# A conditioned block on one core: the first pair of batches in another order, weight sums stored in front of the last rows and x, and the last inner sum split over VectorE's queue

## The chip, the cores and the metric

The kernel runs on one core of a Trainium2 chip. The metric is the device time of one execution in microseconds; before the change the median of three runs is 465.22 us (464.73 to 466.36). The profile is of a further execution of its own, which took 467.79 us.

The engines are named as in the profile: PE is TensorE (matmuls; PEld its weight loads), DVE is VectorE, ACT is ScalarE, POOL is GpSimd, and SP is SyncE, which here only issues DMAs. A small q behind an engine (SPq, ACTq) marks its sequencer.

## What is computed

x has 32 batches of 128 tokens with 512 features, in float32. Each batch has a condition vector, from which two small products give a shift, a scale and a gate for each of two halves. The first half acts on masked tokens only; the second half acts on all tokens.

```python
m = mask[:, :, None]
emb = silu(t) @ ada_w + ada_b
shift, scale, gate_msa = split(emb, 3, axis=1)
norm = layernorm(x) * (1.0 + scale[:, None]) + shift[:, None]
norm = where(m, norm, 0.0)
fwd = gelu(norm @ ssm_w1 + ssm_b1) @ ssm_w2 + ssm_b2
bwd = flip(the same with bwd_w1 .. bwd_b2 on flip(norm, axis=1), axis=1)
x = x + gate_msa[:, None] * where(m, fwd + bwd, 0.0)
ff_ada = silu(t) @ ffada_w + ffada_b
shift_mlp, scale_mlp, gate_mlp = split(ff_ada, 3, axis=1)
ff_norm = layernorm(x) * (1.0 + scale_mlp[:, None]) + shift_mlp[:, None]
h = gelu_tanh(ff_norm @ ff_w1 + ff_b1)        # 512 -> 1024
out = x + gate_mlp[:, None] * (h @ ff_w2 + ff_b2)   # 1024 -> 512
```

The products act on each token alone, so the two flips cancel, and forward and backward become one product with the two weights side by side.

## The kernel before

**First half, on slots.** The masked tokens are counted and given numbers, the slots. Rows of x are gathered into 512 slots (four tiles of 128, `xc`), in two halves of 256. For each half, `hidden` (L182) computes eight tiles of gelu outputs, `project` (L196) multiplies them into one accumulator of 128 slots (eight matmuls, L202), and `keep_slots` (L299) does the rest: VectorE adds the bias (L208), multiplies by the gate (L210), adds `xc` (L301), and SP stores the rows in `x1_rows` in DRAM (L302). Slots 0 and 1 are done early. Slots 2 and 3 are computed while the second half of the kernel begins.

**Second half, in four pairs.** A pair is two sides of four batches (1024 tokens). x is loaded by SP into tiles of two batches (`load_side`, L325; the DMA is L331), and `take_first_half` (L671) then overwrites masked tokens by indirect gathers from `x1_rows` on GpSimd (L675), one for each batch; other tokens are out of bounds and stay. VectorE takes statistics (L707, L708), GpSimd the root (L713), VectorE normalises (L719) and transposes blocks of 32 by 32 in place. `turned` (L739) then brings features onto partitions with 16 DMAs of 64 KB in pieces of 128 bytes (L746), and `scaled` (L748) applies scale and shift by batch on ScalarE (L729, 16 instructions a side). In pair 0, side 1 is turned by TensorE (L735) and scaled by VectorE (L727) instead, between the matmuls of `project` for slot 3.

**Seven products instead of eight, twice.** Both products of a pair are done by Strassen's method in Winograd's form. In the first one it is used on two levels. The outer level has streams 1 to 7 (`STREAMS` gives the order 1, 2, 5, 6, 3, 7, 4). Within each, the products P1 to P7 are matmuls with 128 rows of contraction (L907), with sums taken in PSUM and by VectorE, GpSimd and ScalarE on the way. The outer sums of weights for streams 5, 6, 7 and 4 are made once by `weight_sums` (numbered 1, 2, 3 and 4), stored in DRAM (`t_rows`) by `store_weight_sums` (L586, DMAs L588 and L589, 512 and 384 KB), and loaded again for each pair by `load_weights` (L848, DMA L853). The inner sums of x are `TokenBlocks` (L757): `one(1)` to `one(4)` (L776), each one VectorE instruction of 128x1024. The outer sums of x are `token_sums` (L826: L836, L840, L843, L846).

`FirstProduct.phase` (L898) issues the matmuls of one product and what follows from it. What matters here:

- `seed` (L947) prepares the accumulator e from a: a ScalarE copy (L953) for stream 1, a VectorE sum (L951) for stream 2. P2 waits for it.
- After P6, VectorE puts a + P5 into e (L932). P7 and P3 follow.
- After P7 and P4, VectorE makes L937 and L942; after P2 and P3, ScalarE copies (L965) or applies gelu (L869).
- GpSimd makes the sums that cross streams: `with_p5` (L958) and `after` (L987), and `late_sum` (L991).

`SecondProduct` (L1015) does the second product on one level with the steps of `ORDER` (P1U, P5U, P1V, P5V, P2U, ...), 16 matmuls each (L1087). P5 needs block sums of gelu outputs: `first_block` (L1038, L1041), then for P6 the second block, which subtracts `ha` (L1106).

**What sets the order.** Each engine runs its instructions in the order in which the program lists them (the scheduler is set to manual at L364), and an instruction waits on semaphores for what it reads and for buffers to come free. DMAs of SP, ScalarE and GpSimd are issued from the engine's own queue, so a DMA that waits holds up everything behind it there. In steady state the order comes from `window` (L996), which runs the seven products of a new stream mixed with the last of the old, and from `fills`, a table of (window, place) with the functions to be called there. In pair 0 it is written out by hand (L1132 to L1211). Buffers come from pools: the pools `hp` and `gp` of the second half are opened only at L1185, in the space of the pool `ssm` of the first half, so their first writers (the weights' DMA L853 and the first writers of the gelu tiles) wait until the last reader of the tiles there is done.

The order around the change, by hand: five gathers of pair 0, statistics, three more gathers, the DMA of gate rows, the stores of weight sums 4 on GpSimd (L1132 to L1141); the transposes and DMAs of xT on SP and ScalarE, the table load, the 16 scalings; slot 2; slot 3 with the transposes of side 1 between its matmuls (L1173); the stores of weight sums 1 and 2 on SP and two x tiles of pair 1 (L1174, L1175); `one(1)`; slot 3's sum with `one(2)` and `one(3)` between L208 and L210; then the products.

Of the kernel before, what the change touches and what calls it, by code (L numbers as in the profile page):

```python
# [22 lines left out]
def kernel(  # L23
# [158 lines left out]
    def hidden(xT, n, w, bcol, func, name, pool, parts=range(HC)):  # L182

        h = []
        for f in parts:
            ph = ps_h.tile([P, 512], F32, tag="h", name=f"ph_{name}_{f}")
            for k in range(KC):
                nc.tensor.matmul(  # L188
                    ph[:, :n], w[:, k, ts(f, P)], xT[:, k, :], start=(k == 0), stop=(k == KC - 1)
                )  # L190
            t = pool.tile([P, n], F32, tag="h", name=f"h_{name}_{f}", bufs=HC + 2)
            nc.scalar.activation(t, ph[:, :n], func, bias=biasT[:, bcol + f : bcol + f + 1])  # L192
            h.append(t)
        return h
# [10 lines left out]
    def gated(po, bias, gate, name, between=lambda: None):  # L205

        t = tp.tile([P, D], F32, tag="t", name=f"t_{name}")
        nc.vector.tensor_tensor(t, po, bias, ALU.add)  # L208
        between()
        nc.vector.tensor_tensor(t, t, gate, ALU.mult)  # L210
        return t
# [84 lines left out]
    def finish_slots(at, h1, gate, between=None):  # L296
        keep_slots(at, project(at % (NC // 2), h1, w2, f"s{at}", between), gate)

    def keep_slots(at, po, gate, between=lambda: None):  # L299
        t = gated(po, b2, gate, f"s_{at}", between)  # L300
# [100 lines left out]
    slot_row = ssm.tile([P, NS], F32, name="slot_row")  # L401
# [184 lines left out]
    def store_weight_sums(*which, queue=nc.sync):  # L586
        for j in which:
            queue.dma_start(t_rows[j - 1, :, :4], t_sum[j][0])  # L588
            queue.dma_start(t_rows[j - 1, :, 4:], t_sum[j][1][:, :3])  # L589
# [76 lines left out]
    t = in_blocks(sp.tile([P, G, D], F32, tag="s12", name="tw_4"))  # L666
    t_sum[4] = [t[:, :4], t[:, 4:]]
# [347 lines left out]
    class SecondProduct:  # L1015
# [31 lines left out]

        def third_block(self, c):
# [20 lines left out]
        def step(self, step):  # L1069
# [33 lines left out]
            if product == "P5":  # L1103
                self.p5[c] = keep_and_seed((e, a), f"o{p}_{c}")

                nc.vector.tensor_tensor(s1[c], s1[c], ha[:, :hh, tok], ALU.subtract)  # L1106
# [25 lines left out]
    take_first_half(0, x_of[0], range(G + 1))  # L1132
    stats = [Statistics(x_of[0][side], f"0_{side}") for side in range(2)]
# [7 lines left out]
    store_weight_sums(4, queue=nc.gpsimd)  # L1141
# [24 lines left out]

    po_s2 = project(0, h1, w2, "s2")

    def keep_and_turn():
        keep_slots(2, po_s2, gs[0])  # L1170
        turn(2)()

    po = project(1, h1, w2, "s3", {0: turn(0), 1: turn(1), 2: keep_and_turn, 4: turn(3)})  # L1173
    store_weight_sums(1, 2)  # L1174
    x_of[1] = [load_side(1, 0, spare)]  # L1175
    of_x[0] = TokenBlocks(0, xT)
    of_x[0].one(1)

    def outer_sums():
        of_x[0].one(2)  # L1180
        of_x[0].one(3)

    keep_slots(3, po, gs[1], outer_sums)
# [6 lines left out]
    now.apart(1)  # L1190
    now.do(1, "P1")
# [3 lines left out]
    of_x[0].one(4)  # L1195
# [16 lines left out]
    for p in range(NP):  # L1212
# [25 lines left out]
        if more_pairs:  # L1238
            if p == 0:
                x_of[1].append(load_side(1, 1))  # L1240
# [19 lines left out]
            if p == 0:  # L1260
                put(2, 6, take_first_half, 1, x_next, range(2 * G))
            else:
                put(1, 6, take_first_half, p + 1, x_next, range(G))
                put(2, 6, take_first_half, p + 1, x_next, range(G, G + 2))
                put(3, 4, take_first_half, p + 1, x_next, range(G + 2, G + 3))
                put(5, 4, take_first_half, p + 1, x_next, range(G + 3, 2 * G))
# [16 lines left out]
        now.do(4, "P7")  # L1283
        if more_pairs:
            for i in range(2, G):
                blocks(0, i)
            to_feature_rows(0, nc.sync)
        second.step(1)
        now.do(4, "P4")
        second.load_gate(1)  # L1290
        for lo in (0, 2):
            second.first_block(1, lo, lo + 2)
# [169 lines left out]
```

## Time and profile before

| | us |
|---|---|
| Median of three runs (range) | 465.22 (464.73 to 466.36) |
| The profiled execution | 467.79 |
| Its span, first to last instruction | 466.0 |
| Busy in the span: PE / DVE / ACT / POOL | 451.4 / 330.8 / 175.4 / 160.0 |
| First matmul of the first half's last hidden stage | 59.08 |
| First matmul of pair 0's products | 88.42 |
| First matmul of pair 0's second product | 135.61 |
| First matmul of pair 1's products | 180.22 |

A line of a timeline gives start, length (of the whole run of like instructions), engine, line, operation, out<-in with the program's names, shape and count; in brackets the idle time of the engine before it, and what ended it. Matmuls are pipelined, so the start of a group says more than its end. A matmul of float32 shows as two records for each pair of operands, four in a group of two matmuls. In the windows view each row is a stretch of time, with the busy time and the number of instructions of PE, PEld, DVE, ACT and POOL, then the granted clock of TensorE, the mean busy share of the 16 DMA engines and GB/s.

### The profile page before, as it was taken

The page shows a single profiled execution, that of the slowest core. Times are in us where ns is not written, and L with a number is a line of the kernel's source. Part 1 is how long each engine was busy: PE and PEld are TensorE (multiplying, and loading weights), DVE is VectorE, ACT ScalarE, POOL GpSimd, SP SyncE. Part 2 cuts the span into 40 slices and gives each one's busy share as a digit, 9 for nine tenths or more (in the row PEclk, how much of TensorE's full clock was granted, in tenths as well). Part 3 has the DMA queues.
Part 4 walks back from the last instruction along what each step waited for, and adds up shares of the span by engine and source line. Part 5 has one row for each costly group of instructions (what it writes and reads, how often), then busy time and mean ns, then how long its engine had stood idle before and what let it go on. Part 6 is the DMA issues. An engine that isn't in the chain of part 4 may idle for free.

```text
span 466.0 us, 5828 instructions
## 1 busy us (share of the span) xinstructions
PE 451.4 (97%) x2000; PEld 365.3 (78%) x2000; DVE 330.8 (71%) x538; ACT 175.4 (38%) x380; POOL 160.0 (34%) x153
## 2 busy tenths in 40 slices
PE   6899999899999999999999999999999999999995
PEld 2385385477788888888888888888888888888884
DVE  4649768969668759996787399867864995434645
ACT  3121021734364371354553713444546144562000
POOL 6210074038973000389710004897000025660000
PEclk9999999989999999999999999999999999999999
DMA  8999716880406752834086438330973342212022
GB/s 277 386 407 355 302 50 140 265 316 22 165 0 198 102 108 86 291 118 162 1 209 101 98 107 313 98 136 3 235 100 73 127 168 79 80 68 114 0 79 105
DMA packets 82418, 70.41 MB, mean 151 GB/s; under 512 B 63168, under 2 KB 63696, under 8 KB 81362
## 3 DMA queue, kind: packets, MB, share of 16 engines
q1 hardware_dynamic: 67298, 57.03, 40.0%
q0 software_dynamic: 4480, 11.66, 7.4%
q10 hardware_dynamic: 10608, 1.32, 2.0%
q8 instruction: 17, 0.28, 0.3%
q14 instruction: 15, 0.12, 0.1%
HBM read 56.83 MB, written 13.17 MB: 150 GB/s over the span
## 4 chain that ended last, share of the span: by engine, by line
PE 74%; POOL 8%; ACT 5%; issue 5%; DVE 4%; DMA 3%; SPq 0%; POOLq 0%; DVEq 0%
PE a_o L1087 19%; PE e_o L1087 16%; PE a_m L907 14%; PE e_m L907 11%; PE ph_s L188 6%; PE po_s L202 4%; POOL hb L991 2%; ACT hb L869 2%; POOL x L675 2%; DMA x<-in_x_dram 2%; DMA tw<-t_rows 1%; POOL ha L958 1%; DVE xT L727 1%; ACT ha L869 1%; PE part_s L283 1%
## 5 line engine op out<-in xcount | busy, mean ns | idle before, releaser
L958 POOL TENSOR_TENSOR ha<-p_m,ha 128x512 f32<-128x512 f32 x20 | 27.4, 1369 | 152.5 <-ACT ha L965 143.3
L1087 PE MATMUL e_o<-fw,ha 128*128 128x256 f32 x256 | 57.9, 379 | 0.0
L729 ACT ACTIVATE xT<-xT,modT 128x128 f32<-128x128 f32 x112 | 44.2, 480 | 29.4 <-DMA xT<-xn 29.4
L1087 PE MATMUL a_o<-t,hb 128*128 128x256 f32 x240 | 54.1, 379 | 0.0
L1087 PEld LDWEIGHTS e_o<-fw,ha 128*128 128x128 f32 x256 | 48.6, 190 | 6.6
L1087 PEld LDWEIGHTS a_o<-t,hb 128*128 128x128 f32 x240 | 45.6, 190 | 6.2
L675 POOL DMA_INDIRECT x<-x_rows,slot_i x32 | 37.5, 1173 | 26.9 <-DMA x_rows<-t_s 18.6
L869 ACT ACTIVATE hb<-hb,biasT 128x256 f32<-128x256 f32 x64 | 29.0, 501 | 28.1 <-POOL hb L991 19.4
L958 POOL TENSOR_TENSOR hb<-p_m,hb 128x512 f32<-128x512 f32 x20 | 28.3, 1415 | 23.0 <-DVE e_m L951 22.7
L921 ACT COPY p_m<-e_m 128x512 f32<-128x512 f32 x27 | 15.8, 586 | 50.1 <-PE e_m L907 50.1
L1087 PE MATMUL e_o<-fw,s 128*128 128x256 f32 x128 | 29.2, 381 | 0.5 <-DVE s L1041 0.3
L965 ACT COPY ha<-e_m 128x512 f32<-128x512 f32 x32 | 18.5, 579 | 28.5 <-PE e_m L907 26.9
L1087 PE MATMUL a_o<-fw,ha 128*128 128x256 f32 x128 | 28.9, 379 | 0.0
L1087 PE MATMUL a_o<-t,s 128*128 128x256 f32 x128 | 28.9, 379 | 0.0
L202 PE MATMUL po_s<-w,h_s 128*128 128x512 f32 x64 | 28.6, 592 | 0.0
L188 PE MATMUL ph_s<-xT_s,w 128*128 128x256 f32 x128 | 28.6, 382 | 0.0
L1087 PEld LDWEIGHTS e_o<-fw,s 128*128 128x128 f32 x128 | 24.1, 190 | 4.8 <-DVE s L1041 1.7
L188 PEld LDWEIGHTS ph_s<-xT_s,w 128*128 128x128 f32 x128 | 24.0, 190 | 4.7 <-ACT h_s L192 1.5
L1087 PEld LDWEIGHTS a_o<-t,s 128*128 128x128 f32 x128 | 24.3, 190 | 3.3
L1087 PEld LDWEIGHTS a_o<-fw,ha 128*128 128x128 f32 x128 | 24.3, 190 | 3.3
L932 DVE TENSOR_TENSOR e_m<-a_m,ha 128x512 f32<-128x512 f32 x20 | 13.9, 696 | 17.6 <-POOL ha L958 7.4
L869 ACT ACTIVATE ha<-e_m,biasT 128x256 f32<-128x256 f32 x48 | 20.1, 469 | 15.8 <-PE e_m L907 8.9
(207 smaller groups left out, 872.3 us busy)
## 6 DMA issues: line engine op xcount, KB each, us to landing
tw<-t_rows SPq DMA_DIRECT2D x16, 896.0 KB, 5.1
x<-in_x_dram SPq DMA_DIRECT2D x16, 512.0 KB, 6.8
gate<-gate_rows POOLq DMA_DIRECT2D x8, 1024.0 KB, 5.3
out_dram<-x SPq DMA_DIRECT2D x15, 512.0 KB, 3.3
xT<-xn SPq DMA_DIRECT2D x92, 64.0 KB, 2.8
fw<-in_L_cond_ff_w_dram SPq DMA_DIRECT2D x2, 2048.0 KB, 10.4
ada_f<-in_L_cond_ffada_w_dram SPq DMA_DIRECT2D x4, 768.0 KB, 15.4
ada_a<-in_L_cond_ada_w_dram SPq DMA_DIRECT2D x4, 512.0 KB, 7.0
```

Source lines behind the costliest of these rows:

```text
L188: nc.tensor.matmul(ph[:, :n], w[:, k, ts(f, P)], xT[:, k, :], start=(k == 0), stop=(k == KC - 1))
L202: nc.tensor.matmul(po, h[f][:, ts(i, P)], w[:, f, :], start=(f == 0), stop=(f == HC - 1))
L675: nc.gpsimd.indirect_dma_start(out=xs[i // G][i % G // 2][:, i % 2], out_offset=None, in_=x1_rows[:slots, :], in_offset=bass.IndirectOffse ...
L729: nc.scalar.activation(out, src, AF.Identity, bias=shift, scale=scale)
L869: nc.scalar.activation(dst[:, n], src[:, n], AF.Gelu_apprx_tanh, bias=biasT[:, f : f + 1])
L907: nc.tensor.matmul(bank[:, ts(n, QT)], self.w_block(j, product)[:, ts(n, P)], self.x_block(j, product), start=(product in ("P1", "P5") and ...
L921: nc.scalar.copy(p5, e)
L932: nc.vector.tensor_tensor(e, a, p5, add)
L958: nc.gpsimd.tensor_tensor(self.place(RESULT[j], c), self.p5[j], other, ALU.add)
L965: nc.scalar.copy(self.place(RESULT[j], c), src)
L991: nc.gpsimd.tensor_tensor(part, self.place("21", c), part, ALU.add)
L1087: nc.tensor.matmul(part, src[:, k, ts(i, P)], w[product][:, k, :], start=(last and k == 0), stop=True, skip_group_check=True,)
```

## The change

- Pair 0's stores: weight sums 1 leave by GpSimd's queue behind the fifth gather; weight sums 4, which left there behind the eighth, leave by SP with weight sums 2. Sums 4 are written to two other tiles (`s4`, and one that shares its space with `slot_row`). Each store sends its smaller part first.
- The weights of streams 5 and 6 are loaded on SP behind these stores; the last rows of the first half and all four x tiles of pair 1 follow.
- Slot 2: bias, then the block of side 1's scaling that stood behind, then gate, x and store. Slot 3: bias and gate together behind `one(1)`; `one(2)`, `one(3)` and `one(4)` follow, and the sum with x and the store come behind the products P1 to P6 of stream 1.
- The gathers of pair 1 are spread over four places of the table as for the other pairs, instead of eight in one place.
- In each pair, at the start of the second product: the second half of `first_block(1)` and two normalised blocks come ahead of their former place, the second block of U (L1106 before) behind `first_block(1)`.
- The tiles of `hidden` have 8 buffers instead of 10. (A function `gated` loses its argument `between`.)

```diff
--- before.py
+++ after.py
@@ -188,7 +188,7 @@
                 nc.tensor.matmul(
                     ph[:, :n], w[:, k, ts(f, P)], xT[:, k, :], start=(k == 0), stop=(k == KC - 1)
                 )
-            t = pool.tile([P, n], F32, tag="h", name=f"h_{name}_{f}", bufs=HC + 2)
+            t = pool.tile([P, n], F32, tag="h", name=f"h_{name}_{f}", bufs=HC)
             nc.scalar.activation(t, ph[:, :n], func, bias=biasT[:, bcol + f : bcol + f + 1])
             h.append(t)
         return h
@@ -202,11 +202,10 @@
             nc.tensor.matmul(po, h[f][:, ts(i, P)], w[:, f, :], start=(f == 0), stop=(f == HC - 1))
         return po
 
-    def gated(po, bias, gate, name, between=lambda: None):
+    def gated(po, bias, gate, name):
 
         t = tp.tile([P, D], F32, tag="t", name=f"t_{name}")
         nc.vector.tensor_tensor(t, po, bias, ALU.add)
-        between()
         nc.vector.tensor_tensor(t, t, gate, ALU.mult)
         return t
 
@@ -293,11 +292,8 @@
         nc.scalar.copy(t, gate)
         return t
 
-    def finish_slots(at, h1, gate, between=None):
-        keep_slots(at, project(at % (NC // 2), h1, w2, f"s{at}", between), gate)
-
-    def keep_slots(at, po, gate, between=lambda: None):
-        t = gated(po, b2, gate, f"s_{at}", between)
+    def finish_slots(at, h1, gate):
+        t = gated(project(at % (NC // 2), h1, w2, f"s{at}"), b2, gate, f"s_{at}")
         nc.vector.tensor_tensor(t, t, xc[at], ALU.add)
         nc.sync.dma_start(x1_rows[ts(at, P), :], t)
 
@@ -398,7 +394,7 @@
         pattern=[[1, P]],
         channel_multiplier=-1,
     )
-    slot_row = ssm.tile([P, NS], F32, name="slot_row")
+    slot_row = ssm.tile([P, 6 * P], F32, tag="row", name="slot_row")[:, :NS]
     nc.gpsimd.iota(
         slot_row,
         pattern=[[1, NS]],
@@ -585,8 +581,8 @@
 
     def store_weight_sums(*which, queue=nc.sync):
         for j in which:
+            queue.dma_start(t_rows[j - 1, :, 4:], t_sum[j][1][:, :3])
             queue.dma_start(t_rows[j - 1, :, :4], t_sum[j][0])
-            queue.dma_start(t_rows[j - 1, :, 4:], t_sum[j][1][:, :3])
 
     def count_more():
 
@@ -663,8 +659,10 @@
 
     fb2_step = const.tile([P, D // 2], F32, name="fb2_step")
     nc.vector.tensor_tensor(fb2_step, fb2[:, D // 2 :], fb2[:, : D // 2], ALU.subtract)
-    t = in_blocks(sp.tile([P, G, D], F32, tag="s12", name="tw_4"))
-    t_sum[4] = [t[:, :4], t[:, 4:]]
+    t_sum[4] = [
+        in_blocks(sp.tile([P, KC // 2, G * S], F32, tag="s4", name="tw_4")),
+        ssm.tile([P, 6 * P], F32, tag="row", name="tw_4_b").rearrange("p (b f) -> p b f", b=3),
+    ]
     weight_sums(4)
 
 
@@ -1045,6 +1043,12 @@
                 ALU.add,
             )
 
+        def second_block(self, c):
+
+            nc.vector.tensor_tensor(
+                self.s1[c], self.s1[c], self.ha[:, : HC // 2, self.cols[c]], ALU.subtract
+            )
+
         def third_block(self, c):
 
             hh, tok = HC // 2, self.cols[c]
@@ -1066,7 +1070,7 @@
             b = (2 * self.p + side) * G + 2 * c
             nc.sync.dma_start(out[b : b + 2].rearrange("b s d -> s b d"), self.xs[side][c])
 
-        def step(self, step):
+        def step(self, step, late=False):
             p, ha, hb, s1, w = self.p, self.ha, self.hb, self.s1, fw2_of.of
             hh = HC // 2
             product, n = ORDER[step][:2], ORDER[step][2]
@@ -1102,8 +1106,8 @@
                     nc.sync.dma_start(out[(2 * p + 1) * G + 2 * c + i, :, : D // 2], xt)
             if product == "P5":
                 self.p5[c] = keep_and_seed((e, a), f"o{p}_{c}")
-
-                nc.vector.tensor_tensor(s1[c], s1[c], ha[:, :hh, tok], ALU.subtract)
+                if not late:
+                    self.second_block(c)
             elif product == "P2":
                 self.finish(c, 0, 0, e)
 
@@ -1130,6 +1134,7 @@
 
 
     take_first_half(0, x_of[0], range(G + 1))
+    store_weight_sums(1, queue=nc.gpsimd)
     stats = [Statistics(x_of[0][side], f"0_{side}") for side in range(2)]
     xT = [new_xT(0, side) for side in range(2)]
     for i in range(G):
@@ -1138,7 +1143,6 @@
     take_first_half(0, x_of[0], range(G + 1, 2 * G))
     gate_rows = dram.tile([B, D], F32, name="gate_rows")
     nc.gpsimd.dma_start(gate_rows, mod2[2 * B : 3 * B, :])
-    store_weight_sums(4, queue=nc.gpsimd)
 
     def in_turned_blocks(t):
         return t.rearrange("p i d -> p (i d)").rearrange("p (k i c) -> p k i c", i=G, c=P)
@@ -1164,23 +1168,34 @@
     def turn(k):
         return lambda: transposed(1, xn_b, xT[1], k)
 
+    tail = {}
+
+    def with_bias(at, po):
+        tail[at] = tp.tile([P, D], F32, tag="t", name=f"t_s_{at}")
+        nc.vector.tensor_tensor(tail[at], po, b2, ALU.add)
+
+    def with_gate(at, gate):
+        nc.vector.tensor_tensor(tail[at], tail[at], gate, ALU.mult)
+
+    def with_x(at):
+        nc.vector.tensor_tensor(tail[at], tail[at], xc[at], ALU.add)
+        nc.sync.dma_start(x1_rows[ts(at, P), :], tail[at])
+
     po_s2 = project(0, h1, w2, "s2")
 
     def keep_and_turn():
-        keep_slots(2, po_s2, gs[0])
+        with_bias(2, po_s2)
         turn(2)()
+        with_gate(2, gs[0])
+        with_x(2)
 
     po = project(1, h1, w2, "s3", {0: turn(0), 1: turn(1), 2: keep_and_turn, 4: turn(3)})
-    store_weight_sums(1, 2)
-    x_of[1] = [load_side(1, 0, spare)]
+
+    store_weight_sums(4, 2)
     of_x[0] = TokenBlocks(0, xT)
     of_x[0].one(1)
-
-    def outer_sums():
-        of_x[0].one(2)
-        of_x[0].one(3)
-
-    keep_slots(3, po, gs[1], outer_sums)
+    with_bias(3, po)
+    with_gate(3, gs[1])
     first_half.close()
     hp = straight.enter_context(tc.tile_pool(name="hp", bufs=1))
     gp = straight.enter_context(tc.tile_pool(name="gp", bufs=1))
@@ -1188,11 +1203,14 @@
     for j in (1, 2):
         now.load_weights(j)
     now.apart(1)
+    for j in (2, 3, 4):
+        of_x[0].one(j)
     now.do(1, "P1")
     now.seed(1)
     now.do(2, "P1")
     now.do(1, "P2", "P5", "P6")
-    of_x[0].one(4)
+    with_x(3)
+    x_of[1] = load_x(1, spare)
     now.token_sums(1, 0)
     now.do(2, "P5")
     now.do(1, "P7")
@@ -1236,8 +1254,6 @@
         put(6, 5, now.late_gelu, "22")
         put(6, 6, now.late_sum, "21")
         if more_pairs:
-            if p == 0:
-                x_of[1].append(load_side(1, 1))
             x_next = x_of[p + 1]
             stats = [Statistics(x_next[side], f"{p + 1}_{side}") for side in range(2)]
             xn, xT = {}, {}
@@ -1257,13 +1273,10 @@
                 xT[side] = new_xT(p + 1, side)
                 turned(xn[side], xT[side], queues)
 
-            if p == 0:
-                put(2, 6, take_first_half, 1, x_next, range(2 * G))
-            else:
-                put(1, 6, take_first_half, p + 1, x_next, range(G))
-                put(2, 6, take_first_half, p + 1, x_next, range(G, G + 2))
-                put(3, 4, take_first_half, p + 1, x_next, range(G + 2, G + 3))
-                put(5, 4, take_first_half, p + 1, x_next, range(G + 3, 2 * G))
+            put(*((1, 6) if p else (2, 3)), take_first_half, p + 1, x_next, range(G))
+            put(2, 6, take_first_half, p + 1, x_next, range(G, G + 2))
+            put(3, 4, take_first_half, p + 1, x_next, range(G + 2, G + 3))
+            put(5, 4, take_first_half, p + 1, x_next, range(G + 3, 2 * G))
             for i, at in enumerate(((3, 1), (3, 3), (3, 4), (3, 6))):
                 put(*at, stats[0].one, i)
             put(*((3, 6) if p else (5, 4)), stats[0].root)
@@ -1281,15 +1294,17 @@
         now.do(4, "P3")
         second.seed(1)
         now.do(4, "P7")
+        second.first_block(1, 2, 4)
         if more_pairs:
-            for i in range(2, G):
-                blocks(0, i)
+            blocks(0, 2)
+        second.step(1, late=True)
+        now.do(4, "P4")
+        if more_pairs:
+            blocks(0, 3)
             to_feature_rows(0, nc.sync)
-        second.step(1)
-        now.do(4, "P4")
         second.load_gate(1)
-        for lo in (0, 2):
-            second.first_block(1, lo, lo + 2)
+        second.first_block(1, 0, 2)
+        second.second_block(0)
         fill = {5: [lambda: second.third_block(0)], 7: [lambda: second.third_block(1)]}
 
         def put(step, f, *args):
```

## The prediction

> **What bounds the kernel now.** I read the page first (busy shares, the forty slices, the chain that ended last), then the timeline of TensorE with its idle times, then the timelines of the engines that end those idle times.
>
> ```profile
> span 466.0 us, 5828 instructions
> PE 451.4 (97%) x2000; PEld 365.3 (78%) x2000; DVE 330.8 (71%) x538; ACT 175.4 (38%) x380; POOL 160.0 (34%) x153
> ...
> PEclk9999999989999999999999999999999999999999
> ```
>
> TensorE has work in 97% of the span, so only its gaps and its slow stretches can be won. Slice 8 (81.6 to 93.2 us) is the first with a clock below 9 tenths. The timeline of TensorE there (start, length, line, tiles, count, idle before):
>
> ```profile
> 88.42 1.03 PE L907 MATMUL a_m_alone<-xT,fw 128*128 128x256 f32 x4
> 89.77 1.10 PE L907 MATMUL a_m<-xT,fw 128*128 128x256 f32 x4 [0.33 <-DVE t_s L208]
> 92.40 1.59 PE L907 MATMUL e_m<-xT,fw 128*128 128x256 f32 x4 [1.52 <-ACT e_m L953]
> 93.78 1.91 PE L907 MATMUL e_m_alone<-s,fw 128*128 128x256 f32 x4
> 95.49 1.46 PE L907 MATMUL a_m_alone<-s,t 128*128 128x256 f32 x4
> 96.78 1.03 PE L907 MATMUL e_m<-s,fw 128*128 128x256 f32 x4
> ```
>
> Four matmuls at full clock start 0.86 us apart (later groups: 101.70, 102.57, 103.43). Here the starts are 1.35, 2.63, 1.38, 1.71 and 1.29 apart: this is where the first pair loses time. The idle 1.52 us ends with ScalarE's copy at L953. The half rate after it is the clock; the windows view says so (last three columns: clock, DMA share, GB/s):
>
> ```profile
> 89.50:92.90 3.40, 1.60 (x6) 1.16 (x7) 3.37 (x5) 2.85 (x8) 0.00 (x0) 1.00 1.01 344
> 92.90:96.30 3.40, 3.40 (x9) 2.71 (x9) 0.32 (x1) 1.16 (x2) 0.00 (x0) 0.50 0.96 323
> ```
>
> What made ScalarE late is on its own timeline, and what made that late on GpSimd's:
>
> ```profile
> 73.49 10.31 ACTq L746 DMA_DIRECT2D xT<-xn  x8
> 83.84 1.28 ACT L1152 ACT_TABLE_LOAD   x1 [10.24 <-DMA xT<-xn]
> ...
> 85.60 6.26 ACT L729 ACTIVATE xT<-xT,modT 128x128 f32<-128x128 f32 x16 [0.27 <-DMA xT<-xn]
> 91.77 0.57 ACT L953 COPY e_m<-a_m_alone 128x512 f32<-128x512 f32 x1
> ```
> ```profile
> 73.07 0.60 POOL L588 DMA_DIRECT2D t_rows<-tw  x1
> 73.67 0.54 POOL L589 DMA_DIRECT2D t_rows<-tw  x1
> ...
> 115.31 0.99 POOL L675 DMA_INDIRECT x<-x_rows,slot_i  x1 [0.30 <-issue]
> 116.32 1.28 POOL L958 TENSOR_TENSOR ha<-p_m,ha 128x512 f32<-128x512 f32 x1
> ```
>
> The 896 KB of weight sums 4 are issued in the same half microsecond as the first pieces of xT. Pieces issued from 73 to 77 us land after a median 5.0 us; those issued from 155 to 157.9 us, with no such store about, after 2.2 us. Sixteen scalings and the copy then follow the last piece. A second, smaller place: eight gathers hold GpSimd from 104.24 to 116.30, and the sums behind them (L958, L987) end VectorE waits of 0.86 and 0.94 us at 117.64 and 120.08.
>
> **What the Trainium skill says.** "DMA: Bandwidth & Descriptors", section "Issuing engines are not separate DMA queues": transfers from all engines end on the same 16 DMA engines and interleave. The trace agrees: 5.0 against 2.2 us. "TensorE: Matmul & The Clock Gate", section "What's actually happening": the clock falls to half after an idle window of about 3.4 us, and the windows run freely. The trace agrees on the length (3.4 us at 0.50) but not on "idle": TensorE was busy 1.60 of 3.40 us in the window before. "SBUF — State Buffer", section "Who interferes with whom": a VectorE operation with two SBUF inputs contends with GpSimd's reads; here the L836 sums beside L958 take about 1.2 instead of 0.68 us. I move none of those.
>
> **The change, part by part.** The profiled execution took 467.79 us (span 466.0 and 1.79 around it), 2.57 above the median 465.22; the sum is made against 467.79.
>
> (a) Weight sums 1 (two stores) now leave GpSimd behind the fifth gather, at 65.72; sums 4 leave it and go to SP. Two issues cost 0.60 + 0.54, so GpSimd reaches the root L713 at 66.9; its input is ready at 67.2: nothing, with 0.3 us of cover. Behind them wait three gathers, needed by VectorE at 74.2 at the earliest and landing near 73.6 at worst. DMA is idle there (share 0.06 from 66 to 73.4), and 917 KB at the 300 GB/s that such stores reach take 3 us, done by 71. So xT starts free. First pieces should land at 73.5 + 2.2 = 75.7 instead of 78.8; the sixteen took 6.7 us from first landing to last; so the last lands at 82.4 to 83.7 (taking the slower pace of 8.2 us of transfer) instead of 85.5. I take 83.3. ScalarE's table load hides as before. The copy L953 starts 6.2 us later, at 89.5, and ends at 90.1. TensorE's next group can start when a_m is through: 89.77 + 0.86 = 90.63 instead of 92.40. **1.75 us.** If pieces gain only 1 us, 0.9 of it is left.
>
> (b) With 0.3 us idle left in the window there is no reason for the half clock. From 92.40 to 96.78 three groups took 4.38 instead of 2.59: **1.75 us**. The windows run freely, so a timed run need not have lost this; bounds 0 and 1.75.
>
> (c) VectorE's order. The last inner sum keeps its place at 88.94 (L208), its product with the gate moves up, outer half 4 moves in front of L932, the sum with x behind it. From 88.94: 0.6, 0.7, then three halves at 1.14 end at 93.7. TensorE, now early, reaches P6 of product 1 at 92.4 to 93.25, so L932 starts at 93.7, 0.2 late; P7 starts at 94.4. VectorE then has x, sx, hb (L937) and e_m (L951): 96.7, and P2 of product 2 starts at 96.8, 0.7 after TensorE is free. Before: 100.73. Total so far 3.9, so this part gives 3.9 - 3.5 = **0.4 us**. Outer half 4 also waits for store 4, issued on SP near 87.2: plus a median 3.2 to 3.9 us makes 91, before it is needed at 92.6.
>
> (d) SP. In front of the last rows and x: store 4, store 2, weights 1 and 2. Weights 1 wait for the gate product (90.3) and so leave near 90.5 instead of 93.82, need 3 to 5 us, and are used at 103.43 - 3.9 = 99.5: cover 4 us. Last rows leave at 95 instead of 93.25, the four x tiles behind them at 95.4 to 98 instead of 89.22 to 96.5. From 86 us on 6.2 MB at 370 GB/s keep the DMA full until about 103.5, as now; x lands at 99 to 103.5. The first gather follows GpSimd's sums at 100.4. Cost: nothing to 1 us, taken as nothing.
>
> (e) Six gathers instead of eight stand before L958: 2 x 1.5 = 3 us less. GpSimd is then at 109.4 where TensorE wants the sum at 112. The waits go that make TensorE lose 0.24 before 118.39 and 0.71 before 120.83: **0.95 us**. Gathers 7 and 8 follow later sums; GpSimd's idle 2.70 us before 134.41 takes the last.
>
> (f) Junction of each pair: half of the first block moves ahead of its step, the second block behind it. TensorE's P5V waits (0.3 us at 148.87, 0.15 idle at 240.16 and 331.83) for a last gelu that ends eight ScalarE operations without a gap from 142.73; that order is unchanged: 0. New is VectorE's wait for ScalarE from 142.9 to 143.6; with the block itself the last transpose ends at 147.4 instead of 145.3. Behind it queue 28 xT pieces. Cover: they share DMA with two gate copies until 151.5 and SP then issues one per 0.67 us; and outer half 1 ends at 176.8, 269.2 and 360.4 where TensorE starts at 180.2, 271.4 and 363.0 (slack 3.4, 2.2, 2.6). Taken as 0; uncovered it would cost up to 2.1 a pair.
>
> (g) Fewer h buffers, the shared slot row and the two-part tile of sums 4: reuse long after the last reader (matmuls end at 53.3, h is rewritten at 61.0). 0.
>
> Sum: 1.75 + 1.75 + 0.4 + 0.95 = 4.85, so 462.9 for the profiled execution. Against the median I count (b) at a quarter, since 465.22 lies 2.57 below the profiled time and may have lost it only in part: 1.75 + 0.45 + 0.4 + 0.95 = 3.55, **461.7 us**.
>
> **The rivals.** *The wait moves to VectorE or to x*: TensorE finds L951 or a gather late. For it: VectorE is full from 97 to 117, x is issued up to 6 us later. Against it: the slack in (d) and (e). It costs (e) and 0.7 us more: 463.3. *xT is not earlier*: pieces of 128-byte elements have their own pace, and if the store cost only a start in the queue, (a) and (b) shrink to 0.3; with half of (e) lost too: 464.5, no change. *Slower*: the junction. If xT reaches ScalarE as late as the last transpose plus a wait behind the second gate copy, it is not the delay that counts but what exceeds the slack: from 2.2 us on TensorE waits at the start of a pair; 5 us late costs 1.6 + 2.8 + 2.4 = 6.8 over three pairs: 461.7 + 6.8 = 468.5. Against it: issue pace and gates hide most of 2.1 us.
>
> **How the numbers follow.** Forecast 0.64; VectorE or x 0.18; xT not earlier 0.13; slower 0.05. A change of 0.3% (1.4 us) is about what a measurement of this kernel can tell. Faster 0.82, same 0.13, slower 0.05. The range reaches from the full sum with (b) and 0.6 us beyond (459.8) up to 464.2, which takes in the second case and part of the third.
>
> **What would show it.** Right: TensorE's e_m group near 90.7 without an idle of 1.5 us, no half clock behind it; the first scaling L729 (L727 after) near 83.4; P2 of product 2 near 96.8; no GpSimd wait at L932 before P6's sums; starts of the later pairs all shifted by one amount. Wrong: scaling still at 85, a GpSimd gather waiting for x, or TensorE idle at 180, 271 or 363 less the shift.

## The result, and the profile after

| | before | after |
|---|---|---|
| Median of 22 executions each, alternating | 465.76 us (464.73 to 468.08) | 465.44 us (462.67 to 466.94) |
| Ratio, with its 95% interval | | 0.9982 (0.9965 to 0.9998) |
| The profiled execution (its span) | 467.79 (466.0) | 463.40 (461.7) |

The change gives 0.3 us in the median, where 3.5 were forecast, and 465.44 lies above the range. The two profiled executions differ by 4.4 us, but they are no typical pair: the one of before is slower than 21 of its 22 timed runs, and the one of after is the fourth fastest of its 22. Each single reading below has to be held against the medians.

The page of after (busy lines and clock), against the 451.4 us of PE and the single 8 in slice 8 of before:

```profile
span 461.7 us, 5825 instructions
...
PE 448.6 (97%) x2000; PEld 364.2 (79%) x2000; DVE 332.1 (72%) x538; ACT 175.2 (38%) x380; POOL 157.8 (34%) x153
...
PEclk9999999999999999999999999999999999999999
```

TensorE at the start of the products (timeline, as in the prediction; in after L905, L930, L949 and L956 are L907, L932, L951 and L958 of before):

```profile
89.12 1.10 PE L905 MATMUL a_m<-xT,fw 128*128 128x256 f32 x4
90.06 1.03 PE L905 MATMUL e_m<-xT,fw 128*128 128x256 f32 x4
...
93.84 1.13 PE L905 MATMUL a_m_alone<-xT,t 128*128 128x256 f32 x4 [0.17 <-DVE e_m L930]
...
96.36 1.13 PE L905 MATMUL e_m<-xT,fw 128*128 128x256 f32 x4 [0.53 <-DVE e_m L949]
```

The idle 1.52 us ahead of e_m is gone, and P2 of stream 2 starts at 96.36 instead of 100.73. The window behind it (engines, then clock 1.00, DMA share, GB/s) has full clock where before had 0.50:

```profile
92.90:96.30 3.40, 2.77 (x12) 1.78 (x10) 3.37 (x7) 1.01 (x2) 0.01 (x1) 1.00 0.96 325
```

The cause is on ScalarE's timeline, as forecast: the pieces of xT are issued by 80.5 instead of 83.8, and the scalings start 2.73 us sooner (0.46 of it because everything from the first half's last stage on is that much earlier in this execution).

```profile
73.11 7.42 ACTq L744 DMA_DIRECT2D xT<-xn  x8
80.57 1.28 ACT L1156 ACT_TABLE_LOAD   x1 [7.37 <-DMA xT<-xn]
...
82.87 6.27 ACT L727 ACTIVATE xT<-xT,modT 128x128 f32<-128x128 f32 x16 [0.80 <-DMA xT<-xn]
89.03 0.58 ACT L951 COPY e_m<-a_m_alone 128x512 f32<-128x512 f32 x1
```

New is a wait of GpSimd ahead of its first gather for pair 1, which the prediction named as a sign of its being wrong:

```profile
97.99 1.72 POOL L956 TENSOR_TENSOR ha<-p_m,ha 128x512 f32<-128x512 f32 x1
102.35 1.37 POOL L673 DMA_INDIRECT x<-x_rows,slot_i  x1 [2.65 <-DMA x<-in_x_dram]
...
110.66 1.27 POOL L956 TENSOR_TENSOR ha<-p_m,ha 128x512 f32<-128x512 f32 x1
```

and pair 1, which is not shifted but longer: from its first group a_m<-xT,fw to the same of pair 2 TensorE takes 92.40 us (176.15 to 268.55) against 91.30 before.

### The profile page after: what moved, and what is told of

The parts are those of the page before. It is cut to its first block, busy times and chain, and to the rows that moved or that the text cites. A ratio compares the mean times of both kernels' runs of the same rounds, so it can differ in the third digit from the quotient of the medians.

```text
span 461.7 us, 5825 instructions
## 1 busy us (share of the span) xinstructions
PE 448.6 (97%) x2000; PEld 364.2 (79%) x2000; DVE 332.1 (72%) x538; ACT 175.2 (38%) x380; POOL 157.8 (34%) x153
## 4 chain that ended last, share of the span: by engine, by line
PE 69%; DVE 9%; ACT 7%; POOL 5%; SPq 4%; issue 4%; DMA 1%; POOLq 0%; ACTq 0%; DVEq 0%
PE a_m L905 15%; PE a_o L1091 14%; PE e_m L905 12%; PE e_o L1091 12%; PE ph_s L188 6%; PE po_s L202 4%; SPq L744 4%; POOL hb L989 2%; ACT hb L867 2%; ACT xT L727 1%; DVE sx L834 1%; DVE xT L725 1%; ACT ha L867 1%; DVE xn_sy L838 1%; PE part_s L282 1%
## 5 line engine op out<-in xcount | busy, mean ns | idle before, releaser
L956 POOL TENSOR_TENSOR ha<-p_m,ha 128x512 f32<-128x512 f32 x20 | 26.9, 1345 | 152.5 <-ACT ha L963 143.3
L673 POOL DMA_INDIRECT x<-x_rows,slot_i x32 | 36.4, 1136 | 28.7 <-DMA x_rows<-t_s 18.1
L956 POOL TENSOR_TENSOR hb<-p_m,hb 128x512 f32<-128x512 f32 x20 | 28.2, 1409 | 20.4 <-DVE hb L935 20.1
L930 DVE TENSOR_TENSOR e_m<-a_m,ha 128x512 f32<-128x512 f32 x20 | 13.9, 697 | 16.6 <-POOL ha L956 6.6
```

What stands on the lines that cost most here:

```text
L673: nc.gpsimd.indirect_dma_start(out=xs[i // G][i % G // 2][:, i % 2], out_offset=None, in_=x1_rows[:slots, :], in_offset=bass.IndirectOffse ...
L930: nc.vector.tensor_tensor(e, a, p5, add)
L956: nc.gpsimd.tensor_tensor(self.place(RESULT[j], c), self.p5[j], other, ALU.add)
```

## The stages of all the profiled executions

Since single executions differ by up to 5 us, the traces are compared by stage. The columns are differences of TensorE's starts on its timeline, in us: A from the first product (a_m_alone) to P2 of stream 1, B on to P2 of stream 2, C on to the second product of pair 0, D from the first group a_m<-xT,fw of pair 1 to that of pair 2. The last column is the distance from P2 of stream 2 to the sum on GpSimd (L958, in the changed kernel L956) behind the gathers.

| kernel | A | B | C | D | to the sum |
|---|---|---|---|---|---|
| before | 3.98 | 8.34 | 34.88 | 91.30 | 15.59 |
| before, second execution | 4.07 | 6.65 | 34.89 | 91.38 | 15.59 |
| changed | 2.10 | 6.30 | 34.48 | 92.40 | 14.30 |
| changed, again | 2.10 | 6.30 | 34.47 | 92.50 | 14.28 |
| changed, old junction | 2.10 | 6.30 | 36.10 | 92.35 | 15.93 |
| changed, x ahead | 2.11 | 6.30 | 37.38 | 91.39 | 17.22 |
| changed, old junction, rows first | 2.10 | 7.03 | 34.49 | 91.28 | 14.30 |
| the same, with x ahead | 2.11 | 7.03 | 34.25 | 91.29 | 13.00 |
| the same, outer half 4 behind | 2.10 | 6.55 | 33.92 | 91.34 | 12.99 |
| before + stores | 2.30 | 6.81 | 34.90 | 91.30 | 15.60 |
| before + stores + spread gathers | 2.29 | 6.81 | 33.92 | 91.35 | 12.99 |
| the same, again | 2.30 | 6.81 | 33.92 | 91.29 | 12.98 |
| before + junction | 3.99 | 6.65 | 34.89 | 91.62 | 15.60 |
| before + junction, second execution | 3.91 | 8.34 | 34.90 | 91.42 | 15.60 |

## The experiments

The first four ran together, then the next four, then the last four, each group beside its own runs of the kernel before (75, 43 and 59 of them; medians 465.84, 466.12 and 465.83). Each has 22 executions of its own, except the first run of the stores with the spread gathers, which has 6, and the second executions of the kernel before and of the junction alone, which are one profiled execution each. A "loss" of TensorE ahead of a group is the distance of the two starts less the 0.86 us that a group of four matmuls takes at full clock.

**The changed kernel again.** No edit.

> The changed kernel once more, to see in a second trace what its executions differ in (they took 462.7 to 466.9 us). Theory X: where an execution is slow, the x tiles of pair 1, which now leave SP last, land late, GpSimd's first gather waits longer than the 2.65 us of the first trace, and TensorE waits at L930 or L949 near 112 to 116 us. Theory J: the junction leaves xT of the next pair without slack, and a slow execution has TensorE idle or VectorE behind at the start of pairs 1 to 3 (near 175, 268, 359 us). Median expected 465.2 either way.

466.47 us, ratio 1.0002 (0.9984 to 1.0020). So 0.9982 and 1.0002 are two measurements of one thing: the change is worth between nothing and some 0.3%. The profiled execution, 464.44 us, is again the fourth fastest of its 22. In it the first gather waits 1.90 us, and TensorE loses 0.44 and 0.24 us ahead of P2 of stream 2 in pairs 1 and 3. What a typical, slower execution of the changed kernel loses is in no trace here; it is inferred from the kernels below.

**The old order at the junction.**

```diff
-        second.first_block(1, 2, 4)
-        if more_pairs:
-            blocks(0, 2)
-        second.step(1, late=True)
+        if more_pairs:
+            for i in range(2, G):
+                blocks(0, i)
+            to_feature_rows(0, nc.sync)
+        second.step(1)
...
```

> The changed kernel with the old order at the start of the second product in every pair; the rest of the change stays. Theory J: the three pairs lose nothing, median 462.5 to 463.5. Theory X: as the changed kernel, 465.2.

465.36 us, ratio 0.9989 (0.9973 to 1.0006): below the changed kernel beside it by 0.6 us by the ratios and 1.1 by the medians, with intervals that overlap, and level with the first measurement of the changed kernel (0.9982). Its trace shows where else the gain can be lost. On GpSimd the first gather waits as in the changed kernel, and two of the six are long:

```profile
102.34 1.23 POOL L673 DMA_INDIRECT x<-x_rows,slot_i  x1 [2.46 <-DMA x<-in_x_dram]
...
105.29 2.43 POOL L673 DMA_INDIRECT x<-x_rows,slot_i  x1 [0.31 <-issue]
108.02 1.83 POOL L673 DMA_INDIRECT x<-x_rows,slot_i  x1 [0.30 <-issue]
...
112.47 1.28 POOL L956 TENSOR_TENSOR ha<-p_m,ha 128x512 f32<-128x512 f32 x1
```

TensorE then waits for the VectorE sums that need GpSimd's, as it did before the change:

```profile
114.54 1.13 PE L905 MATMUL e_m<-xn_sy,tw 128*128 128x256 f32 x4 [0.31 <-DVE e_m L930]
...
116.98 1.13 PE L905 MATMUL e_m<-xT,fw 128*128 128x256 f32 x4 [0.45 <-DVE e_m L949]
...
121.91 1.13 PE L905 MATMUL e_m<-s,fw 128*128 128x256 f32 x4 [0.34 <-DVE e_m L930]
```

**x ahead of the weights.** The first two x tiles of pair 1 directly behind the stores.

```diff
     store_weight_sums(4, 2)
+    x_of[1] = [load_side(1, 0, spare)]
     of_x[0] = TokenBlocks(0, xT)
...
     with_x(3)
-    x_of[1] = load_x(1, spare)
+    x_of[1].append(load_side(1, 1))
```

> The changed kernel with the first two x tiles of pair 1 loaded directly behind the stores, in front of the weights of streams 5 and 6, as before the change; the other two stay behind the last rows. Theory X: the first gather no longer waits, median 462.5 to 463.5. Theory J: as the changed kernel, 465.2.

467.38 us, ratio 1.0026 (1.0012 to 1.0041): slower. The theory in its simple form, that x itself lands too late, fell. The first gather waits longer, and for something else: the last rows, which it reads and which now land at 103.64.

```profile
104.52 1.12 POOL L673 DMA_INDIRECT x<-x_rows,slot_i  x1 [4.61 <-DMA x_rows<-t_s]
```

**The stores alone.** The kernel before, with weight sums 1 and 4 exchanged between the queues (and the smaller part of each store first, the tiles for it, 8 buffers). Nothing else.

```diff
     take_first_half(0, x_of[0], range(G + 1))
+    store_weight_sums(1, queue=nc.gpsimd)
...
-    store_weight_sums(4, queue=nc.gpsimd)
...
-    store_weight_sums(1, 2)
+    store_weight_sums(4, 2)
```

> The kernel before with only the stores exchanged (sums 1 by GpSimd behind the fifth gather, sums 4 by SP, the tiles that this needs). The prediction's steps (a) and (b): the scaling L729 starts near 83.3 instead of 85.6, TensorE's idle 1.5 us before P2 goes, and the half clock with it: 1.75 us faster, 463.9 to 464.1, up to 3.5 where the half clock fell into the kernel before. If (a) is of no use: 465.7.

464.17 us, ratio 0.9966 (0.9951 to 0.9981): 1.7 us less than before, and less than both measurements of the changed kernel. Column A has it: 2.30 instead of 4.0.

**The stores and the spread gathers,** with SP's order as before.

```diff
-            if p == 0:
-                put(2, 6, take_first_half, 1, x_next, range(2 * G))
-            else:
-                put(1, 6, take_first_half, p + 1, x_next, range(G))
+            put(*((1, 6) if p else (2, 3)), take_first_half, p + 1, x_next, range(G))
...
```

> The kernel before with two parts of the change: the stores (as in the run of the stores alone) and the gathers of pair 1 spread over four places. SP's order of weights, last rows and x stays as in the kernel before. Theory 'SP order': spreading the gathers is worth the 0.95 us of step (e) as long as the first gather does not wait for x: first gather at 101.1 without a wait, VectorE's sums behind L958 on time, TensorE without the two idle times at 115 to 118; about 463.2 us, 2.6 less than before, 1.0 less than with the stores alone (464.2). Rival 'the gathers cost nothing that isn't lost again elsewhere': as with the stores alone, 464.2.

463.39 us in 6 executions, ratio 0.9943 (0.9920 to 0.9965).

> The kernel before with the stores and the spread gathers once more, for more runs than the six of the first time. If the 463.4 us of those hold: 0.57% less than before. If they were six good ones: 464.2, as with the stores alone, and the spread of the gathers is worth nothing.

463.87 us, ratio 0.9956 (0.9943 to 0.9969). So 0.5% holds, and it beats both kernels. On GpSimd (line numbers 2 higher here) the first gather starts without a wait, and the sum stands 13.0 us behind P2 of stream 2:

```profile
98.50 1.71 POOL L960 TENSOR_TENSOR ha<-p_m,ha 128x512 f32<-128x512 f32 x1
100.38 1.12 POOL L677 DMA_INDIRECT x<-x_rows,slot_i  x1 [0.17 <-issue]
...
109.86 1.29 POOL L960 TENSOR_TENSOR ha<-p_m,ha 128x512 f32<-128x512 f32 x1
```

Column C is 33.92 against 34.90 with the stores alone: 0.98, where step (e) said 0.95.

**The junction alone,** on the kernel before.

```diff
+        second.first_block(1, 2, 4)
         if more_pairs:
-            for i in range(2, G):
-                blocks(0, i)
-            to_feature_rows(0, nc.sync)
-        second.step(1)
+            blocks(0, 2)
+        second.step(1, late=True)
...
```

> The kernel before with the new order at the start of each second product and nothing else. Theory 'junction': the last pieces of xT leave about 2.5 us later in each pair, outer half 1 ends with 1.9 us less slack or none, and VectorE behind it lets TensorE wait some tenths in the first products of pairs 1 to 3: 0.9 to 1.1 us longer than before, 466.8. Rival, as the prediction put it: the slack covers all of it, 0, 465.8.

467.40 us, ratio 1.0025 (1.0013 to 1.0038): 1.2 us more. In its profile TensorE loses only 0.15 us ahead of P2 of stream 2 in pair 1, where the kernel before loses 0.03 in both its executions, so this profile hardly shows the cost. A second one follows.

> A second profiled execution of the kernel before with the new order at the start of the second products alone. Theory 'the junction costs some tenths in some pairs, not in each': TensorE loses 0.2 to 0.4 us more than in the kernel before ahead of P2 and P7 of stream 2 in one or two of pairs 1 to 3 (in the first look: 0.05 us more, in pair 1), with outer half 1 ending 2 us ahead of TensorE instead of 2.7. Rival 'it is a wait for weights from memory': TensorE loses up to 1 us ahead of products that read these weights, and nothing ahead of P2 and P7.

468.15 us. TensorE loses 0.17 us there in pair 1 and 0.63 in pair 3 (before: 0.03 in each), and nothing that waits for weights:

```profile
377.47 1.13 PE L907 MATMUL e_m<-xT,fw 128*128 128x256 f32 x4 [0.47 <-DVE e_m L951]
```

The theory holds in its place; the size differs from pair to pair, and of the 1.2 us of the times the two profiles show 0.1 and 0.7. In this execution the half clock is there too (0.97 and 0.53 in the two windows from 89.5 to 96.3).

**The last rows first.** The changed kernel with the old junction, and with slot 3's sum and store behind the gate product instead of behind P6.

```diff
     with_gate(3, gs[1])
+    with_x(3)
...
     now.do(1, "P2", "P5", "P6")
-    with_x(3)
     x_of[1] = load_x(1, spare)
```

> The changed kernel with the old order at the start of each second product, and the last rows stored directly behind the product with the gate, ahead of the weights of streams 5 and 6. Compare with the changed kernel with the old order alone (465.4). Theory 'the last rows': SP stands at the last rows until about 94.5, and x and the gathers that read these rows come late because of that; with the rows at about 92, x leaves from about 92.5 instead of 94.8, the first gather starts near 101 instead of 102.3, and the time is about 463.7. Rival 'bytes': from 86 to 104 us the DMA is full, and what is moved to the end of the line lands at the same time in any order; the first gather still waits for x until 102 or more, 465.4. Rival 'VectorE': the sum with x ahead of outer halves 2 to 4 delays L932 by 0.6 us and P7 with it; 0.6 more, 466.

464.40 us, ratio 0.9962 (0.9950 to 0.9975): 0.0027 or 1.3 us less than with the rows late (0.9973 to 1.0006; the ends of the intervals overlap by 0.0002). SP's queue shows what moved. With the rows first:

```profile
90.93 0.32 SPq L1182 DMA_DIRECT2D x_rows<-t_s  x1
91.56 1.99 SPq L851 DMA_DIRECT2D tw<-t_rows  x2
93.60 2.11 SPq L327 DMA_DIRECT2D x<-in_x_dram  x4
```

and in the changed kernel:

```profile
89.97 3.84 SPq L851 DMA_DIRECT2D tw<-t_rows  x2
94.40 0.32 SPq L1182 DMA_DIRECT2D x_rows<-t_s  x1
94.77 2.72 SPq L327 DMA_DIRECT2D x<-in_x_dram  x4
```

There the second weights' load waits until 93.48 (for store 2, which lands at 93.4), and rows and x stand behind it. The theory was wrong in part: in this execution too the first gather waits for x (1.56 us, to 102.39). And the rival "VectorE" is also right: the earlier sum costs 0.73 us in column B. But that moves TensorE back, and the sum on GpSimd is again 14.30 behind P2 of stream 2, without further loss.

**Rows and x both early,** so that SP's order is that of before but for the last two tiles (the edits of the last run and of "x ahead" together).

> The changed kernel with the old order at the start of each second product, the last rows directly behind the product with the gate (as in the run with the rows first), and the first two x tiles of pair 1 directly behind the stores. SP's order is then stores, x, rows, weights, x, as in the kernel before but for the place of the last two tiles. Theory 'SP order': with the rows not held back, x ahead does no harm to the gathers; the first gather starts without a wait for x near 101, GpSimd is back 1 us sooner than with the rows first and x behind, and the waits of 0.19 and 0.17 us at 121 to 123 go: 464.0, against 464.4 with the rows first alone. Rival 'x ahead is bad in itself', as where x went ahead of rows and weights with the rows late (1.1 us slower than the changed kernel): 465.5.

464.23 us, ratio 0.9957 (0.9943 to 0.9972). The first gather starts at 101.19 with no wait; the sum is at 13.00. So x ahead is bad only where the rows are late. That x ahead is better than x behind, once the rows are first, is shown in this trace but not in the times (0.9957 against 0.9962).

**Outer half 4 behind P6.** The last kernel, with `one(4)` back where it was.

```diff
-    for j in (2, 3, 4):
+    for j in (2, 3):
         of_x[0].one(j)
...
     now.do(1, "P2", "P5", "P6")
+    of_x[0].one(4)
```

> As the kernel with rows and x early, and outer half 4 of pair 0 goes back behind VectorE's sum a + P5 of stream 1, where it was before the change. Theory 'VectorE': the sum starts one half (1.14 us) sooner, so that the 1.0 us which TensorE loses ahead of P7 of stream 1 falls to about 0.4; P2 of stream 2 stays where VectorE's queue puts it: 0 to 0.6 us less than the kernel with rows and x early, 463.4 to 464.0. Rival 'no gain, since VectorE works without a pause up to the sum for stream 2 and only the order within that stretch changes': the same as the kernel with rows and x early.

463.71 us, ratio 0.9961 (0.9949 to 0.9974): column B falls from 7.03 to 6.55, the times cannot tell it from the last.

**The kernel before, a second profiled execution.**

> The kernel before, for a second profiled execution. Theory 'the half clock at 92.9 to 96.3 belongs to one execution': here the clock is full in that window, the three groups behind ScalarE's copy start 0.86 us apart, and pair 1 starts 1.5 to 1.8 us sooner than in the first profile (at 178.5 instead of 180.2). Rival 'the idle time before it brings it each time': half clock again and 180.2.

465.29 us. The first group of pair 1 starts at 177.66, where the first execution has it at 180.05: 2.4 us sooner, where 1.5 to 1.8 were said, and 0.8 of that lies ahead of the products. The clock is full, with an even longer idle time (1.61 us) ahead of it:

```profile
92.90:96.30 3.40, 3.40 (x16) 2.54 (x14) 1.66 (x2) 1.76 (x3) 0.00 (x0) 1.00 0.98 354
```

So the half clock doesn't follow each time from the idle time. How often it comes can be estimated from the mean clock that each run lists, since 3.4 us at half clock take about 0.004 off it: of the 177 runs of before, 36 have a mean of 0.996 or less, and they take some 1.8 us more than the rest (467.75, 467.5 and 467.5 on average against 465.75, 465.9 and 465.6 in the three groups). Of the 182 runs of the kernels here that have the new stores, 12 do. Such a window can also lie elsewhere: in the first execution of the junction alone it lay from 15.6 to 19.0. What the change takes away is at most the difference of the two shares.

## Why the prediction was wrong

**(a) was right.** 1.75 us said; column A falls by 1.7 to 2.0 in every kernel with the new stores, and the stores alone give 1.7 in the median (with (b)'s average share in it).

**(b) was right in the profile and oversized in the runs.** It is worth 1.69 us when it happens (8.34 against 6.65). Runs with such a window are 36 of 177 before and 12 of 182 after: about (0.20 - 0.07) x 1.8 = 0.25 us on average, where 0.45 was counted. The error is 0.2 us.

**(c) was right.** Column B falls to 6.30, from 6.65 without the half clock, and from 6.81 with the stores alone; said 0.4. P2 of stream 2 came at 96.36, said 96.8.

**(d) failed: "Cost: nothing to 1 us, taken as nothing".** The prediction let x leave from 95.4 and land at "99 to 103.5", and had GpSimd begin gathering at 100.4, so that nothing would wait. That gives the first tile, which the first gather reads, 3.6 us from issue to landing. In the traces of the changed kernel it took 6.7 and 6.0: issued at 94.77 and 94.96, it landed at 101.5 and 100.93, and the gather started at 102.35 and 101.78, after waits of 2.65 and 1.90 us. The first profile of before already had the time that these four tiles need beside the other transfers (the last figure of the line, a median in us):

```profile
x<-in_x_dram SPq DMA_DIRECT2D x4, 512.0 KB, 7.3
```

**(e) failed with it.** "GpSimd is then at 109.4" (12.6 us behind P2 of stream 2): it was at 110.66, which is 14.30. The table has what that costs. With six gathers, 13.0 gives 33.92 in column C (34.25 in the kernel with rows and x early), 14.30 gives 34.48, 15.93 gives 36.10, and 17.22 gives 37.38: beyond 14.3 each 1 us of GpSimd's lateness is 1 us of TensorE (1.63 more gives 1.62, 1.29 more gives 1.28). So the changed kernel works at the edge. In its two profiled executions it got 0.4 of the 0.95; with the old junction, otherwise the same, two long gathers turned the gain into a loss of 1.2. The times point the same way: the four ratios with the rows late are 0.9982, 1.0002, 0.9989 and 1.0026, the six with the rows early and the new stores lie from 0.9943 to 0.9966. But three of the four have the new junction too, and none of the six has it, so one pair alone separates the rows from the junction: the old junction with the rows late and with the rows first. By it the place of `with_x(3)`, which bought the gain of (c), cost 1.3 us (0.9962 to 0.9989, with intervals that just touch, and that although the early sum pays 0.73 us in B). Whether it is VectorE's sum or SP's store of it that counts was not separated, since one waits for the other.

**(f) failed: "Taken as 0".** The new order costs 1.2 us (0.6 to 1.8) on the kernel before; on the changed one it isn't resolved, since the old order gave 0.9989 there and the new one 0.9982 and 1.0002. The slack of "3.4, 2.2, 2.6" us was measured from the end of outer half 1 to TensorE's start of the pair (for pair 1 the timeline has that start at 180.05, which makes 3.2). That isn't the slack that counts, since VectorE works from outer half 1 to the sum ahead of P2 of stream 2 nearly without a pause. Its timeline in the second execution of before, where the only pause is 0.30 us (0.87 in the first):

```profile
173.78 1.23 DVE L776 TENSOR_TENSOR s<-xT 128x1024 f32<-128x1024 f32 x1 [4.86 <-ACT xT L729]
...
188.22 0.69 DVE L1061 TENSOR_TENSOR t_o<-a_o,gate 128x512 f32<-128x512 f32 x1 [0.30 <-PE a_o L1087]
...
190.76 0.69 DVE L951 TENSOR_TENSOR e_m<-a_m,ha 128x512 f32<-128x512 f32 x1
```

and in the changed kernel, where there is none:

```profile
172.14 1.22 DVE L774 TENSOR_TENSOR s<-xT 128x1024 f32<-128x1024 f32 x1 [5.60 <-ACT xT L727]
...
188.73 0.69 DVE L949 TENSOR_TENSOR e_m<-a_m,ha 128x512 f32<-128x512 f32 x1
189.33 1.59 DVE L838 TENSOR_TENSOR xn_sy<-sx,xT 128x512 f32<-128x512 f32 x1
```

Outer half 1 starts 4.75 us ahead of the first group a_m<-xT,fw in that execution of before (178.53 - 173.78; 5.31 in the first), 4.01 ahead in the changed kernel (176.15 - 172.14), 4.22 and 4.21 in the two executions of the junction alone. From outer half 1 to the sum VectorE takes 16.98 us before and 16.59 in the changed kernel, so it has 0.39 to spare. The 0.74 us less that (f) leaves it are more than that, and the rest is the 0.34 us more that TensorE loses ahead of P2 there (0.37 against 0.03). The first piece of xT leaves 2.15 us later than before in the junction alone, the last one only 0.5 to 1.1: the issue pace hides most, as said; the rest is no longer hidden by anything. The other two losses in pair 1 are 0.27 ahead of P7, behind a VectorE sum of 1.59 instead of 0.68 us, and 0.37 ahead of stream 6, which waits for its weights; the latter is no part of the junction, for it is 1.07 with the old order.

**(g) was right**: nothing there waits.

**The sum.** The two parts that were costed right and don't depend on (d) and (f) are (a) and (e), 2.70; the kernel that has just these, with (b)'s average share, is 2.0 and 2.7 us faster than before (0.9956 and 0.9943). What the changed kernel adds costs 1.3 us for the late rows with (c) in it (give or take 1.0), and 1.2 for the junction (give or take 0.6): -0.5 to 0.2 us are left, where the two measurements of it have 0.8 and -0.1. Taking both out of the changed kernel at once, as the kernel with the last rows first does, gains 0.9 to 1.9 us (0.9962 against 0.9982 and 1.0002). A kernel with the rows early and the new junction wasn't run. That the profiled execution of after, 463.40 us, comes close to the 462.9 said for it is luck: its kernel's median is 2 us slower. The rival "the wait moves to VectorE or x" named the right place and was priced at 1.6 us; the rival "junction" was right in kind and, at 6.8 us, over five times too dear. The prediction held them against each other as alternatives; they came together.

What stays open: what a typical execution of the changed kernel loses and where, why a gather takes 1.0 us in one place and 2.43 in another, and how the junction's 1.2 us is shared out between the pairs, since the five profiled executions with it show from nothing to 0.65 us in a pair at P2 and P7 of stream 2.

## What to carry to other kernels

Measure slack to the next instruction that is really waited for, through the queue of the engine between: an engine that has no pause from the delayed instruction to that one has no slack, however long TensorE is busy in between. When an edit moves a small store behind a product, list what stands behind it in its DMA queue and who reads what it stores; here rows of 256 KB held back x and the gathers, and cost more than the VectorE slot they freed. Take a DMA's time to landing from like DMAs beside the same traffic in the profile; here it stood there with 7.3 us, and 3.6 were taken. And where several moves each use up "some tenths" of a margin, add them up in one ledger for that margin.

## What the runs showed of the hardware

- The same idle time can bring the half clock or not: of four profiled executions with an idle time ahead of P2, those with 1.52 and 1.44 us had it behind, those with 1.52 and 1.61 us not. The Trainium skill, "TensorE: Matmul & The Clock Gate", section "What's actually happening", has windows of 3413 ns that run freely. The traces agree: each stretch at one clock that they record, but for the last one, which the end cuts off, lasts a multiple of 3.413 us (3.41, 6.83, 81.92, 368.64, 443.73 and 450.56). In the window that ended where the half clock began TensorE was busy for 1.64 and 1.63 us; in the other two executions, with the windows counted from another change of the clock in the same trace, for 1.80 and 1.71. Four executions make no rule, and once the half clock came behind a window with 2.29 us busy (at 15.6 us, in the first half).
- Loads of 896 KB of weights beside x tiles and gathers took 7.4 us (issued at 191.72, landed at 199.11) and 7.8 us (192.84 to 200.61) where TensorE wanted them after 7. Ten of the fourteen profiled executions lose 0.2 to 1.1 us ahead of a stream that begins with such weights, in one or two of the later pairs, in the old order and the new. It may be a part of the spread of 2 to 6 us in each kernel's runs; no run separates it.
- Six gathers in a row took 8.3 to 10.1 us on GpSimd, from issue to the next instruction, in the same program order.
